# A second attention pass with the second exponential a step later and its product two steps behind

## The chip, the cores and the metric

The kernel runs on one core of a Trainium2 chip. The metric is the device time of one execution in microseconds. It was run three times (3113.05, 3113.25 and 3115.47 us); one more execution was recorded by the hardware profiler. Comparisons below are with the median, 3113.25 us.

## The reference

The program is a small perceiver of four layers. In each layer 128 query tokens of width 256 attend to a long context of 12544 tokens of width 192, then follow a self-attention and a feed-forward part. Only the context attention of layers 0 and 2 is changed. Both compute, with 16 heads of width 16 and a scale of 1/4:

```python
q = x @ Wq;  k = context @ Wk;  v = context @ Wv       # layer 2 adds bq, bk, bv
scores = einsum('bhid,bhjd->bhij', q, k) * scale
scores = where(context_mask, scores, -max)             # layer 0 only
out = einsum('bhij,bhjd->bhid', softmax(scores), v) @ Wo   # layer 2 adds bo
```

Layer 1 does the same with clipped scores, and layer 3 has wider heads and a kernel of its own. All arithmetic is in 32-bit floats.

## The kernel before, in words

`attend_twice_in` handles the context attention of layers 0, 1 and 2. It takes the heads in two groups of eight (`g`). For each group it goes over the context twice. The first pass computes the scores once to find each query's maximum (`highest`, L550 and L551) and, in between, projects the context into keys and values, which stay in SBUF. The second pass computes the scores again, subtracts the maximum, takes the exponential and multiplies by the values. A column of ones beside the values yields the softmax's sum.

The second pass has 49 steps, each of two 128-token chunks. A step has four units (`t`), each with two of the group's heads: 32 rows of the query and key tiles, so that units sit on different rows of the array. In layers 0 and 2 (`weights`, without a clip) the units are treated in two ways:

- Units 0 and 1 go into a PSUM tile of two banks, `pair`. TensorE itself adds the negative maximum (`less_maximum`, L584, in layer 2; in layer 0 the row of the mask does it too, L629). ScalarE then takes the exponential straight from PSUM (L634). I call this the early exponential.
- Units 2 and 3 go into one PSUM bank each, `one`. VectorE subtracts the maximum, and in layer 0 adds the mask, on the way to SBUF: two instructions over 512 columns in layer 2 (L289), four over 256 in layer 0 (L292). ScalarE then takes the exponential in place (L645). I call this the late exponential.

The product with the values is `weighted` (L654): eight matmuls for each half, the first half with the early exponential, the second with the late one. The profile records each of these 32-bit matmuls as two. The product of a step is issued after the scores of the next step. PSUM has two `pair` tiles (four banks), three `one` tiles and one accumulator, all eight banks.

The manager `in_order` makes TensorE, VectorE and ScalarE keep the order in which the code names the work in these passes; elsewhere a scheduler places instructions. An engine runs its instructions in order and stops at the first one whose semaphore isn't ready. Transfers are issued from queues: SP's, and at times GpSimd's.

In layer 0 a mask row is made for every four chunks, so for every two steps, which I call a block. `mask_rows` copies the mask's bytes into four partitions (L533, by SP's queue), and GpSimd turns them into a row (L535, then L537 in the second pass). There are two byte tiles for each pass and three row tiles.

After the steps of group 0, the first keys and values of group 1 are projected before the last product; after group 1 the output is transposed, normalised and projected.

Of the kernel before, what the change touches and what calls it, by code (L numbers as in the profile page):

```python
# [12 lines left out]
F32 = mybir.dt.float32  # L13
# [3 lines left out]
AF = mybir.ActivationFunctionType  # L17
# [4 lines left out]
P = 128  # L22
D = 256
# [3 lines left out]
S2 = 12544  # L27
# [9 lines left out]
RANK = 32  # L37
# [168 lines left out]
class Net:  # L206
# [222 lines left out]
    def layernorm(self, x):  # L429
        nc = self.nc  # L430
        st = self.sp.tile([P, nc.vector.BN_STATS_DIM], F32, tag="bn", name="bn")
        nc.vector.bn_stats(st, x)
        mv = self.sp.tile([P, nc.vector.BN_AGGR_DIM], F32, tag="mv", name="mv")
        nc.vector.bn_aggr(mv, st)
        r = self.stat(1)
        self.ts(r, mv[:, 1:2], 1e-5, None, ALU.add)
        nc.scalar.activation(r, r, AF.Sqrt)
        nc.vector.reciprocal(r, r)
        xn = self.ap.tile([P, D], F32, tag="xn", name="xn")
        self.ts(xn, x, mv[:, 0:1], r, ALU.subtract, ALU.mult)  # L440
        return xn

# [67 lines left out]
    def attend_twice_in(self, pool, o, qz, keys, masked, clip, between):  # L510
        nc, d = self.nc, self.d
# [3 lines left out]
        rows = []  # L515
# [10 lines left out]
        def mask_rows(b, second=False):  # L526


            src = d["mask"].rearrange("c p -> (c p)")[b * SB : min(S2, b * SB + SB)].unsqueeze(0)
            n = src.shape[-1]  # L530
            to = rows8[second][b % 2]
            at = 3 if second else 0
            nc.sync.dma_start(to[at:P:32, :n], src.to_broadcast([4, n]))  # L533
            row = pool.tile([P, SB], BF16, tag="row", name="row", bufs=3)
            nc.gpsimd.tensor_scalar(row[:, :n], to[:, :n], 0.0, 1.0, ALU.is_gt, ALU.subtract)  # L535
            if second:
                nc.gpsimd.tensor_scalar(row[:, :n], row[:, :n], self.bar, three, ALU.mult, ALU.add)  # L537
            else:
                nc.gpsimd.tensor_scalar(row[:, :n], row[:, :n], self.bar, None, ALU.mult)
            return row  # L540
# [49 lines left out]
            at = x[:, j * HB : (j + 1) * HB]  # L590
            nc.tensor.matmul(at, keys.kT(c // 4)[tiles[t], k], q, start=start, stop=True, skip_group_check=True)  # L591

        def exponentials(bufs):
            e = pool.tile([P, 2, 2, 2, P], F32, tag="e", name="e", bufs=bufs)
            return e, e.rearrange("p i j s q -> p i (j s q)")

        def weights_clipped(g, c, m, floor):
# [17 lines left out]
        def weights(g, c, m, less, row):  # L615


            pair = self.pair()
            x = [pair[:, 0, :], pair[:, 1, :], self.single(), self.single()]
            if row is None:  # L620
                for t in range(2):
                    less_maximum(t, x[t], m)
            else:
                for j in range(2):
                    at = slice(j * HB, (j + 1) * HB)
                    k = slice((c % 4 + j) * P, (c % 4 + j + 1) * P)
                    for t in range(2):
                        r = tiles[t]
                        nc.tensor.matmul(x[t][:, at], row[r, k], m[r, at], start=j == 0, stop=False, skip_group_check=True)  # L629
            for j in range(2):  # L630
                for t in range(4):
                    score(g, c, t, j, x[t], start=t >= 2 and j == 0)
            e, to = exponentials(4)
            nc.scalar.activation(to, pair, AF.Exp)  # L634
            es = [e]
            e, to = exponentials(4)
            for i in range(2):
                by_chunk = x[2 + i].rearrange("p (j n) -> p j n", j=2)
                dest = to[:, i].rearrange("p (j n) -> p j n", j=2)
                if row is None:  # L640
                    self.tt(dest, by_chunk, bc(less[:, i], 1, 2), ALU.add)
                    continue
                for j in range(2):
                    self.stt(dest[:, j], by_chunk[:, j], self.mask_col[:, c + j : c + j + 1], less[:, i], ALU.add, ALU.add)
            nc.scalar.activation(to, to, AF.Exp)  # L645
            return es + [e]

        def weighted(g, c, es, acc):

            v = keys.v(c // 4)  # L650
            for half in range(2):
                for j in range(2):
                    for t in range(4):
                        nc.tensor.matmul(  # L654
                            acc[32 * t : 32 * t + 17, half, :], v[:, c % 4 + j, 4 * half + t, :], es[half][:, t // 2, j, t % 2, :],
                            start=c + j + half == 0, stop=c + j == S2 // P - 1, skip_group_check=True,
                        )

        for g in range(2):
            if g == 0:  # L660
# [40 lines left out]
            made, lag = [], 1 if clip is None else 2  # L701
            engines = [mybir.EngineType.PE, mybir.EngineType.DVE, mybir.EngineType.Activation]
            with self.in_order(*(engines if clip is None else [])):
                for c in range(0, S2 // P, 2):
                    if clip is not None:
                        es = weights_clipped(g, c, m, floor)
                    else:
                        if masked and c % 4 == 0:
                            rows.append(mask_rows(c // 4, True))
                        es = weights(g, c, m, less, rows[-1] if masked else None)  # L710
                    made.append((g, c, es, acc))
                    if len(made) > lag:
                        weighted(*made.pop(0))
            if g == 0:
                for b in range(2):
                    for part in range(2):
                        keys.project(1, b, part)
            for step in made:
                weighted(*step)
            oT = pool.tile([P, 2, P], F32, tag="oT", name="oT", bufs=1)  # L720
            nc.vector.tensor_copy(oT, acc)
            p = self.pair()
            for half in range(2):
# [245 lines left out]
    def xattn_biased(self, x, name, guarded, keys):  # L969
        nc, d = self.nc, self.d  # L970
        with self.tc.tile_pool(name=name, bufs=2, reuse_waits="tile") as pool:
            xT = self.normed(x)
            wq = self.load_w(d[f"{name}_Wq"], 2, D, "wq")
            bq = self.load_row(d[f"{name}_bq"], D)
            bv = self.all_rows(d[f"{name}_bv"], D, "bv", pool)
            wo = self.load_w(d[f"{name}_Wo"], 2, D, "wo")
            bo = self.load_row(d[f"{name}_bo"], D)
            qz = pool.tile([P, 2, 2, P], F32, tag="qz", name="qz", bufs=1)
            for g in range(2):
                c = slice(g * P, (g + 1) * P)  # L980
# [51 lines left out]
    def prepare_l3(self, pool):  # L1032
# [25 lines left out]
        def load():  # L1058
            for j, name in enumerate("qkvo"):
                alpha = self.all_rows(d[f"L3_xattn_{name}_alpha"], 1, f"a{name}", self.sp)  # L1060
                self.ts(self.rate[:, j : j + 1], alpha, 1.0 / RANK, None, ALU.mult)
            for i, k in ((1, "k"), (2, "v")):
                down = pool.tile([RANK, 2 * P], F32, tag=f"down{k}", name="down")
                nc.sync.dma_start(down[:, :CD], d[f"L3_xattn_{k}_downT"])
                nc.sync.dma_start(down[:, CD:], d[f"L3_xattn_{k}_downT"][:, P:])
                up = pool.tile([RANK, dims], F32, tag=f"up{k}", name="up")
                nc.sync.dma_start(up, d[f"L3_xattn_{k}_up"])
                w = self.load_kv(d[f"L3_xattn_W{k}"], dims, f"w{k}", own)
                self.w3.append(w)
                parts.append(add_low(i, k, down, up, w))  # L1070
# [743 lines left out]
```

## Time and profile before

| what | us |
|---|---|
| median of three runs | 3113.25 |
| the profiled execution | 3108.01 |
| its span | 3106.3 |
| layer 0, group 0: from the first to the last early exponential's start (171.26 to 288.55) | 117.29 |
| layer 0, group 1 (447.59 to 563.97) | 116.38 |
| layer 2, group 0 (1518.64 to 1628.81) | 110.17 |
| layer 2, group 1 (1783.01 to 1890.68) | 107.67 |
| TensorE busy in these four, in that order | 111.07, 110.73, 109.92, 107.26 |
| ScalarE busy in these four | 94.63, 94.54, 94.70, 94.62 |
| VectorE busy in these four | 79.70, 79.71, 62.02, 61.92 |
| GpSimd busy in these four | 65.26, 58.23, 0, 0 |

A group in the profile is a line with an engine, an operation and its tiles. After the bar stand its busy time in us and the mean of one in ns; after the second bar the idle time of the engine just before these instructions, and what ended most of it. In the timeline a line has its start, its duration, engine, line, operation, tiles and count; square brackets hold the idle time before it. The chain of waits is followed back from the last instruction to whatever released each one; its lines have a start, a duration, and what ran. PE is TensorE, PEld its weight loads, DVE VectorE, ACT ScalarE, POOL GpSimd. The end of a matmul is modelled, so starts are the better witnesses.

### The profile page before, as it was taken

To read this page: it belongs to the slowest core of one execution; us is meant where nothing else is said; L and a number is where in the kernel's file an instruction comes from. 1 tells how busy PE (TensorE), PEld (TensorE's weight loads), DVE (VectorE), ACT (ScalarE), POOL (GpSimd) and SP (SyncE) were. 2 spreads that over 40 slices of the span, in tenths; PEclk is the share of its full clock that TensorE was granted. 3 is DMA by queue.
4 is the path that set the end of the run, shared out by engine and by line. 5 is a ranking of instruction groups with operands and counts; after the bars stand their busy time and mean duration, and the time that the engine had idled before them with its cause. 6 is when DMAs were issued, how large, how long until landed. Compare 5 with 4: busy or idle time off the path is not lost.

```text
span 3106.3 us, 78634 instructions
## 1 busy us (share of the span) xinstructions
PE 2943.0 (95%) x34877; PEld 2201.4 (71%) x34877; DVE 2249.8 (72%) x2887; ACT 1429.1 (46%) x1673; POOL 430.4 (14%) x451
## 2 busy tenths in 40 slices
PE   9999999869999999899999999899999999999979
PEld 6666656535576676675666566489889889889867
DVE  6866876638897898669657755477777777777854
ACT  1166128421284266311482185256555556556521
POOL 6645665212000000120000001000000000000000
PEclk9999999989999999899899999899999999999979
DMA  4100210551101201452102105322223232223436
GB/s 131 55 18 22 71 45 3 182 207 55 32 3 52 60 18 29 130 163 57 34 3 73 55 3 202 120 84 83 84 80 88 81 85 82 84 79 88 122 112 205
DMA packets 165659, 246.97 MB, mean 80 GB/s; under 512 B 20061, under 2 KB 107231, under 8 KB 165320
## 3 DMA queue, kind: packets, MB, share of 16 engines
q1 hardware_dynamic: 160600, 227.77, 24.1%
q0 software_dynamic: 4608, 14.16, 1.4%
q8 instruction: 274, 4.49, 0.6%
q14 instruction: 65, 0.53, 0.1%
q10 hardware_dynamic: 112, 0.01, 0.0%
HBM read 241.75 MB, written 0.13 MB: 78 GB/s over the span
## 4 chain that ended last, share of the span: by engine, by line
PE 80%; DVE 13%; ACT 4%; issue 2%; DMA 1%; POOL 0%; SPq 0%; ACTq 0%; DVEq 0%; POOLq 0%
PE pair L102 20%; PE pair L550 10%; PE v L102 8%; PE acc L654 6%; PE sc L774 6%; PE acc L816 6%; PE ps L278 5%; PE pair L591 5%; DVE e L292 4%; DVE parts L551 3%; PE acc L278 2%; PE kv L102 2%; PE one L591 2%; ACT e L645 2%; PE pair L584 2%
## 5 line engine op out<-in xcount | busy, mean ns | idle before, releaser
L551 DVE TENSOR_REDUCE parts<-pair 128x2 f32<-128x1024 f32 x600 | 679.2, 1198 | 104.4 <-PE pair L550 104.2
L102 PE MATMUL pair<-ctxA,wk 128*128 128x256 f32 x1236 | 328.9, 399 | 1.4 <-ACT kT L193 1.1
L102 PEld LDWEIGHTS pair<-ctxA,wk 128*128 128x128 f32 x1236 | 217.0, 190 | 139.9 <-DVE parts L551 96.0
L550 PE MATMUL pair<-kT,qz 32*128 32x512 f32 (+1 forms) x1632 | 277.5, 615 | 9.2 <-DVE parts L551 8.9
L289 DVE TENSOR_TENSOR top<-top,kept 128x1024 f32<-128x1024 f32 (+2 forms) x145 | 169.1, 1169 | 133.3 <-ACT kept L776 132.0
L776 ACT COPY kept<-sc 128x1024 f32<-128x1024 f32 (+1 forms) x135 | 136.2, 1009 | 259.7 <-PE sc L774 259.7
L645 ACT ACTIVATE e<-e 128x1024 f32<-128x1024 f32 x196 | 207.2, 1057 | 72.6 <-DVE e L292 45.6
L292 DVE SCALAR_TENSOR_TENSOR e<-pair,floor 128x1024 f32<-128x1024 f32 x196 | 230.5, 1219 | 8.3 <-PE pair L591 2.3
L654 PE MATMUL acc<-e,v 128*17 128x128 f32 x6336 | 221.5, 274 | 11.6 <-ACT e L645 10.2
L611 ACT ACTIVATE e<-e 128x1024 f32<-128x1024 f32 x196 | 207.2, 1057 | 40.0 <-DVE e L292 32.5
L292 DVE SCALAR_TENSOR_TENSOR e<-one,maskcol,less 128x256 f32<-128x256 f32 x392 | 162.6, 477 | 78.5 <-PE pair L591 51.4
L591 PE MATMUL pair<-qz,kT 32*128 32x256 f32 x2112 | 219.4, 374 | 0.0
L535 POOL TENSOR_SCALAR row<-mask 128x512 bf16<-128x512 uint8 (+1 forms) x100 | 189.3, 1894 | 209.9 <-PE pair L629 106.4
L654 PEld LDWEIGHTS acc<-e,v 128*17 128x17 f32 x6336 | 145.1, 97 | 97.2 <-issue 42.5
L634 ACT ACTIVATE e<-pair 128x1024 f32<-128x1024 f32 x196 | 197.4, 1007 | 33.0 <-PE pair L591 32.4
L132 ACT ACTIVATE kT<-pair,bk 128x512 f32<-128x512 f32 (+1 forms) x68 | 45.9, 675 | 348.1 <-PE pair L102 348.1
L774 PE MATMUL sc<-qz,kT 64*128 64x128 f32 x2816 | 197.8, 279 | 0.0
L289 DVE TENSOR_TENSOR e<-one,less 128x512 f32<-128x512 f32 x196 | 126.4, 686 | 95.4 <-PE pair L591 92.9
L102 PEld LDWEIGHTS v<-wv,ctxA 128*128 128x128 f32 x1568 | 190.5, 192 | 6.6 <-issue 1.7
L102 PE MATMUL v<-wv,ctxA 128*128 128x128 f32 x1568 | 193.8, 276 | 0.0
L102 PE MATMUL pair<-ctxB,wk 64*128 64x256 f32 x1236 | 188.4, 398 | 0.0
L774 PEld LDWEIGHTS sc<-qz,kT 64*128 64x128 f32 x2816 | 171.6, 187 | 13.0 <-issue 1.3
(438 smaller groups left out, 5465.3 us busy)
## 6 DMA issues: line engine op xcount, KB each, us to landing
ctxA<-in_ctxA SPq DMA_DIRECT2D x324, 256.0 KB
ctxB<-in_ctxB SPq DMA_DIRECT2D x339, 128.0 KB
w<-in_L_ffn_W SPq DMA_DIRECT2D x32, 1024.0 KB
ctxA<-in_ctxA POOLq DMA_DIRECT2D x36, 256.0 KB, 3.4
w<-in_L_ffn_w_gateT SPq DMA_DIRECT2D x8, 1024.0 KB
wu<-in_L_ffn_w_upT SPq DMA_DIRECT2D x8, 1024.0 KB
w<-in_L_ffn_w_downT SPq DMA_DIRECT2D x8, 1024.0 KB
w<-in_L_ffn_w1T SPq DMA_DIRECT2D x8, 1024.0 KB
```

What stands on the lines that cost most here:

```text
L102: self.nc.tensor.matmul(out, a, b, start=start and not low, stop=low == 1, skip_group_check=True)
L278: self.nc.tensor.matmul(out, lhsT, rhs, start=(i == 0), stop=(i == n - 1))
L289: self.nc.vector.tensor_tensor(out, a, b, op)
L292: self.nc.vector.scalar_tensor_tensor(out, a, s, b, op0, op1, **kw)
L550: nc.tensor.matmul(x[:, i, :n], qz[r, g, s, :], keys.kT(b)[r, :n], start=not masked, stop=True)
L551: nc.vector.tensor_reduce(parts[:, s, 2 * half : 2 * half + 2, b], x[:, :, :n], AX.X, ALU.max)
L591: nc.tensor.matmul(at, keys.kT(c // 4)[tiles[t], k], q, start=start, stop=True, skip_group_check=True)
L611: nc.scalar.activation(to, to, AF.Exp)
L634: nc.scalar.activation(to, pair, AF.Exp)
L645: nc.scalar.activation(to, to, AF.Exp)
L654: nc.tensor.matmul(acc[32 * t : 32 * t + 17, half, :], v[:, c % 4 + j, 4 * half + t, :], es[half][:, t // 2, j, t % 2, :], start=c + j + h ...
L774: nc.tensor.matmul(x[:, t, c : c + P], kT[r, c : c + P], qz[r, g, :], start=True, stop=True)
```

## The change

In layers 0 and 2 the late exponential of a step is issued after the early exponential of the next step. The product of a step is split: its first half follows the scores of the next step, its second half those of the step after that. The sums of VectorE get SBUF tiles of their own tag, `late`, three of them; the early exponentials keep two. The second pass's mask bytes go by GpSimd's queue. Some tiles give up room: `xn` has one buffer, the attention's output before the transposition (`oT`) takes the place of `low`, `bv` has one buffer, and two pairs of small matrices for layer 3 (`down`, `up`) share one tile each, on different partitions. Layer 1 keeps its order. What is computed stays the same.

```diff
-            nc.sync.dma_start(to[at:P:32, :n], src.to_broadcast([4, n]))
+            (nc.gpsimd if second else nc.sync).dma_start(to[at:P:32, :n], src.to_broadcast([4, n]))
...
-            e, to = exponentials(4)
+            e, to = exponentials(2)
             nc.scalar.activation(to, pair, AF.Exp)
             es = [e]
-            e, to = exponentials(4)
+            e, to = exponentials(3, "late")
...
-            nc.scalar.activation(to, to, AF.Exp)
             return es + [e]
+
+        def late_exponential(step):
+            to = step[1][1].rearrange("p i j s q -> p i (j s q)")
+            nc.scalar.activation(to, to, AF.Exp)
...
-                        es = weights(g, c, m, less, rows[-1] if masked else None)
-                    made.append((g, c, es, acc))
-                    if len(made) > lag:
-                        weighted(*made.pop(0))
+                    made.append((c, weights(g, c, m, less, rows[-1] if masked else None)))
+                    if n > 0:
+                        late_exponential(made[n - 1])
+                        weighted(0, *made[n - 1], acc)
+                    if n > 1:
+                        weighted(1, *made[n - 2], acc)
+                if clip is None:
+                    late_exponential(made[-1])
             if g == 0:
                 for b in range(2):
                     for part in range(2):
                         keys.project(1, b, part)
-            for step in made:
-                weighted(*step)
-            oT = pool.tile([P, 2, P], F32, tag="oT", name="oT", bufs=1)
+            if clip is not None:
+                weighted(0, *made[-2], acc)
+            weighted(1, *made[-2], acc)
+            for half in range(2):
+                weighted(half, *made[-1], acc)
+            oT = pool.tile([P, 2, P], F32, tag="low" if clip is None else "oT", name="oT", bufs=1)
...
-        xn = self.ap.tile([P, D], F32, tag="xn", name="xn")
+        xn = self.ap.tile([P, D], F32, tag="xn", name="xn", bufs=1)
...
-            bv = self.all_rows(d[f"{name}_bv"], D, "bv", pool)
+            bv = pool.tile([P, D], F32, tag="bv", name="bv", bufs=1)
+            nc.sync.dma_start(bv, d[f"{name}_bv"].to_broadcast([P, D]))
...
+            downs = pool.tile([2 * RANK, 2 * P], F32, tag="down", name="down")
+            ups = pool.tile([2 * RANK, dims], F32, tag="up", name="up")
             for i, k in ((1, "k"), (2, "v")):
-                down = pool.tile([RANK, 2 * P], F32, tag=f"down{k}", name="down")
+                at = slice((i - 1) * RANK, i * RANK)
+                down, up = downs[at], ups[at]
...
-                up = pool.tile([RANK, dims], F32, tag=f"up{k}", name="up")
```

More of the change, by code (lines that the diff above doesn't have):

```diff
@@ L591, in score, with exponentials @@
             nc.tensor.matmul(at, keys.kT(c // 4)[tiles[t], k], q, start=start, stop=True, skip_group_check=True)
-        def exponentials(bufs):
-            e = pool.tile([P, 2, 2, 2, P], F32, tag="e", name="e", bufs=bufs)
+        def exponentials(bufs, tag="e"):
+            e = pool.tile([P, 2, 2, 2, P], F32, tag=tag, name="e", bufs=bufs)
             return e, e.rearrange("p i j s q -> p i (j s q)")
@@ L644, in weights, with weighted @@
                     self.stt(dest[:, j], by_chunk[:, j], self.mask_col[:, c + j : c + j + 1], less[:, i], ALU.add, ALU.add)
+            return es + [e]
+        def late_exponential(step):
+            to = step[1][1].rearrange("p i j s q -> p i (j s q)")
             nc.scalar.activation(to, to, AF.Exp)
-            return es + [e]
-        def weighted(g, c, es, acc):
+        def weighted(half, c, es, acc):
             v = keys.v(c // 4)
[L651 to L657, printed above, removed]
+            for j in range(2):
+                for t in range(4):
+                    nc.tensor.matmul(
+                        acc[32 * t : 32 * t + 17, half, :], v[:, c % 4 + j, 4 * half + t, :], es[half][:, t // 2, j, t % 2, :],
+                        start=c + j + half == 0, stop=c + j == S2 // P - 1, skip_group_check=True,
+                    )
         for g in range(2):
@@ L700, in attend_twice_in @@
             nc.vector.memset(acc, 0.0)
-            made, lag = [], 1 if clip is None else 2
+            made = []
+            steps = range(0, S2 // P, 2)
             engines = [mybir.EngineType.PE, mybir.EngineType.DVE, mybir.EngineType.Activation]
             with self.in_order(*(engines if clip is None else [])):
-                for c in range(0, S2 // P, 2):
+                for n, c in enumerate(steps):
                     if clip is not None:
[L706 to L709, printed above, removed]
-                        es = weights(g, c, m, less, rows[-1] if masked else None)
-                    made.append((g, c, es, acc))
-                    if len(made) > lag:
-                        weighted(*made.pop(0))
+                        made.append((c, weights_clipped(g, c, m, floor)))
+                        if n > 1:
+                            for half in range(2):
+                                weighted(half, *made[n - 2], acc)
+                        continue
+                    if masked and c % 4 == 0:
+                        rows.append(mask_rows(c // 4, True))
+                    made.append((c, weights(g, c, m, less, rows[-1] if masked else None)))
+                    if n > 0:
+                        late_exponential(made[n - 1])
+                        weighted(0, *made[n - 1], acc)
+                    if n > 1:
+                        weighted(1, *made[n - 2], acc)
+                if clip is None:
+                    late_exponential(made[-1])
             if g == 0:
@@ L717, in attend_twice_in @@
                         keys.project(1, b, part)
-            for step in made:
-                weighted(*step)
-            oT = pool.tile([P, 2, P], F32, tag="oT", name="oT", bufs=1)
+            if clip is not None:
+                weighted(0, *made[-2], acc)
+            weighted(1, *made[-2], acc)
+            for half in range(2):
+                weighted(half, *made[-1], acc)
+            oT = pool.tile([P, 2, P], F32, tag="low" if clip is None else "oT", name="oT", bufs=1)
             nc.vector.tensor_copy(oT, acc)
```

## The prediction

> **What bounds the kernel now.** I read the busy shares first, then the costliest groups, then the chain of waits inside one second pass, then TensorE's timeline over one pair of steps. TensorE is busy 95% of the span, so the question is which of its remaining gaps lie in the four passes that change. The groups of those passes:
>
> ```profile
> PE 2943.0 (95%) x34877; PEld 2201.4 (71%) x34877; DVE 2249.8 (72%) x2887; ACT 1429.1 (46%) x1673; POOL 430.4 (14%) x451
> ...
> L645 ACT ACTIVATE e<-e 128x1024 f32<-128x1024 f32 x196 | 207.2, 1057 | 72.6 <-DVE e L292 45.6
> L654 PE MATMUL acc<-e,v 128*17 128x128 f32 x6336 | 221.5, 274 | 11.6 <-ACT e L645 10.2
> ```
>
> The late exponential (L645) idles for VectorE's sum, and the value product (L654) idles for the late exponential. The chain of waits in layer 0's first second pass, here one turn of it:
>
> ```profile
> 224.86 1.67 DVE e L292 x4
> ...
> 226.61 1.07 ACT e L645
> ...
> 227.72 0.63 PE acc L654 x16
> 228.35 0.21 PE pair L629 x2
> ...
> 229.71 1.67 DVE e L292 x4
> ```
>
> One turn is VectorE, ScalarE, half a product, one step's scores, VectorE again: 229.71 - 224.86 = 4.85 us. Only every second VectorE unit appears: a turn covers two steps, so a step costs 2.42, whatever TensorE could do. TensorE's own timeline over that pair:
>
> ```profile
> 226.85 0.63 PE L654 MATMUL acc<-e,v 128*17 128x128 f32 x16
> 227.72 0.63 PE L654 MATMUL acc<-e,v 128*17 128x128 f32 x16 [0.25 <-ACT e L645]
> 228.29 0.28 PE L629 MATMUL pair<-low,row 32*128 32x256 bf16 x2
> 229.47 1.07 PE L654 MATMUL acc<-e,v 128*17 128x128 f32 x32
> 230.48 0.28 PE L629 MATMUL pair<-low,row 32*128 32x256 bf16 x2
> 230.50 0.48 PE L591 MATMUL one<-qz,kT 32*128 32x256 f32 x1
> 230.64 0.48 PE L591 MATMUL one<-qz,kT 32*128 32x256 f32 x1
> 231.69 0.63 PE L654 MATMUL acc<-e,v 128*17 128x128 f32 x16
> ```
>
> In the step that begins at 228.29 the product runs unbroken (x32): 1.18 from step start to product, 1.01 of product, 2.19 in all. In its neighbours the second half waits for the late exponential: 226.85 to 228.29 is 1.44 instead of 1.0. The early exponentials (L634) in the timeline alternate 2.66, 2.19. Layer 2 has the same form with a shorter VectorE unit (1.29 instead of 1.66); its early exponentials alternate 2.29, 2.18, so only 0.11 in two steps is lost.
>
> **What the Trainium skill says.** "TensorE: Matmul & The Clock Gate", Part 1 (the clock gate): after an idle stretch the array runs at half clock until about 3.4 us of activity. The trace agrees: granted clock 0.56 in 445 to 450 us, at a pass's start, and 1.00 in every 5 us from 450 on. So the floor of a step is the full-clock one, and the first steps are priced apart. "DMA: Bandwidth & Descriptors", Anatomy of one DMA: about 2.0 us fixed for a transfer that GpSimd issues; the trace has more, 2.8/3.4/7.0 (min/median/max) to landing for GpSimd's context loads. The same page, SWDGE vs HWDGE vs iDMA: VectorE's 2-port mode can lock GpSimd out while it writes descriptors; "VectorE: DVE Perf Modes", Mode 2x_2P, says that mode needs SBUF operands and a single tensor. Here VectorE's pass work reads PSUM and adds a second tensor, so I expect no lock; no run yet shows it.
>
> **The change, part by part.**
>
> *Late exponential a step later, its product two behind.* Per step TensorE now does scores(n), first half of product n-1, second half of product n-2. Nothing is added or removed: 16 product matmuls a step still, two exponentials on ScalarE, the same VectorE work. What goes is the wait. With T the end of scores(n): VectorE's unit n runs T+0.05 to T+1.7; ScalarE has exp(n) from T+0.05, then the late one of n-1, done by T+2.05. That is wanted after scores(n+1) and half a product, T+2.2+0.5: slack 0.65. The late one of n starts after exp(n+1), near T+3.2, when VectorE has been done for 1.5. ScalarE's start-to-start times are 0.97 (226.61 to 227.58) and 0.90 (1550.35 to 1551.25), 1.87 a step, under 2.19. So TensorE sets the step.
>
> What is late next: the PSUM singles. There are three, two used a step, so a step's second single needs the first single of the step before, free after two of VectorE's four instructions. VectorE starts 1.42 after the step's start (228.29 to 229.71), and the wait above shows the release at 230.64, 0.93 later; the single was wanted at 230.50. That 0.14 moved the product only from 1.18 to 1.21 after the step's start, as other row groups went on. With unbroken products every layer 0 step meets this: 1.21 + 1.0 = 2.21. In layer 2 VectorE's first half is 0.69 and the step is 2.18.
>
> *Buffers.* Early tiles 2, late tiles 3 instead of 4 shared. VectorE's late tile n is the one of n-3, whose product ends just before scores(n); the early tile of n-2 likewise. Covered by the 1.2 of scores; 0.
>
> *Ends.* The first steps have less product, the last ones more. With a loop behind the pass (group 0) half a product, 0.5, moves behind it. In group 1 the last late exponential stands behind two others: it starts 0.97 + 0.96 after the last early one, against 1.70 now in layer 0 (563.97 to 565.67) and 1.32 in layer 2 (1890.68 to 1892.00): +0.2 and +0.6.
>
> *Mask by GpSimd's queue.* 50 transfers leave SP's queue (0.52 each), which is idle then apart from them; behind them stand context loads and, after group 1, the next stage's weights (563.88), which wait for TensorE anyway. On GpSimd they are issued two blocks ahead, right after the row two blocks earlier. GpSimd's cost per block (two steps): 1.92 + 0.77 for the row, 0.1 between, plus 0.54 of issue (its context loads' median): 3.4 of 4.4. Unknown is the issue of this shape; taken 0.54, between 0.5 and 2 (SP's 0.52 to about the skill's fixed cost), hidden either way. Landing has two blocks less that, 8.8 - 3.4 = 5.4, and rows are made some four steps before use:
>
> ```profile
> 226.12 1.92 POOL L535 TENSOR_SCALAR row<-mask 128x512 bf16<-128x512 uint8 x1 [2.05 <-PE pair L629]
> 228.14 0.77 POOL L537 TENSOR_SCALAR row<-row,bar,three 128x512 bf16<-128x512 bf16 x1
> 230.96 1.92 POOL L535 TENSOR_SCALAR row<-mask 128x512 bf16<-128x512 uint8 x1 [2.05 <-PE pair L629]
> ```
>
> GpSimd waits 2.05 in each block for TensorE to free a row. Two such issues (1.1) also go to the program's start, where GpSimd idles 4.5 for the mask; 0. Without cover they would be 1.1.
>
> *The rest* (one xn, oT in the place of low, shared down/up tiles, own bv) keeps every instruction; order on VectorE and on TensorE outside the passes is unchanged. 0; if a shared tile made someone wait, about 1 us each, once.
>
> **The sum**, from first to last early exponential (48 intervals), against the profiled execution. Layer 0, group 0: 117.3 now; then 2.1 + 2.0 for the first two (VectorE and a cold clock set them), 46 x 2.21 = 101.7, and 0.6 for the one irregular step: 106.4, less 10.9, plus 0.5 tail = -10.4. Group 1: 116.4 to 2.1 + 2.0 + 101.7 = 105.8, plus 0.2 = -10.4. Layer 2, group 0: 110.2 to 2.3 + 3.4 (half a cold product, 0.9, gone from 4.28) + 46 x 2.18 = 100.3 + 0.6 = 106.6, plus 0.5 = -3.1. Group 1: 107.7 to 2.7 + 1.7 + 100.3 = 104.7, plus 0.6 = -2.4. Together -26.3: 3108.0 becomes 3081.7. The median of the runs, 3113.25, lies 5.2 above the profiled execution; the saving carried over gives 3087.0.
>
> **Rivals.** *The PSUM single is the new bound.* If the 0.14 wait came through whole, a layer 0 step would be 2.33: 92 x 0.12 = 11 less saved, -15, 3098. For it: the wait is in every second step now, and in all of them after. Against: those steps reach their product 0.03 late, not 0.14. *ScalarE paces it, so that nothing is gained.* In its queue an early exponential waits for scores and the late one stands behind it. It needs over 2.43 a step; 1.87 is measured, and even its two durations end to end are 2.07. Then 3113 within 6. *GpSimd's rows fall behind: slower.* Place: layer 0's row loop. TensorE's mask matmul waits for the row, and everything stands behind it. Layer 2 would still give 5.5, so it decides at a block time of 4.85 + 5.5/49 = 4.96, an issue above some 2.1 us, or a landing that is not covered. With landing exposed, 2.8 + 0.54 + 3.4 = 6.7 a block: 49 x 1.9 = +93, less 5.5, near 3200. For it: GpSimd never carried these. Against: two blocks of prefetch, and 2.05 of spare time.
>
> **How the numbers follow.** Forecast 0.72; single 0.15; ScalarE 0.06; rows 0.07. Faster by over 0.2% (6 us, about what can be told here) 0.87, same 0.06, slower 0.07. The low end has layer 0 steps at 2.19 (-1.8), the irregular steps absorbed (-1.2) and 2 for the spread of the runs: 3082. The high end takes in the single rival with 1 us: 3099.
>
> **What would show it.** Right: early exponentials evenly 2.2 apart in layer 0 and 2.18 in layer 2; the product's wait for the late exponential near nothing; TensorE's wait on singles of 0.1 in every layer 0 step; GpSimd still waiting for TensorE, about 1 us a block. Wrong: an idle of the mask matmul before GpSimd's row; a layer 0 step at 2.3 or more; alternation that remains; a transfer after layer 0 that now ends last.

## The result, and the profile after

The changed kernel takes 3082.51 us (median of four runs, 3080.96 to 3084.20), the kernel before, run beside it, 3114.36 (3113.05 to 3119.38). The ratio is 0.9895, with a 95% interval of 0.9878 to 0.9912. Forecast were 3087.0 and a range of 3082 to 3099. Against the 3113.25 of the forecast the ratio makes 3080.6, so the direction was right and the forecast saving of 26.3 was 5 to 6 us too small. The profiled execution took 3080.96 us with a span of 3079.3, 27.0 under the span before.

The busy shares and the groups of the passes after; a group's columns are busy time, mean ns of one instruction, and the idle time before them with what ended it:

```profile
PE 2923.5 (95%) x34877; PEld 2212.8 (72%) x34877; DVE 2249.7 (73%) x2887; ACT 1428.3 (46%) x1673; POOL 456.7 (15%) x501
...
L658 PE MATMUL acc<-e,v 128*17 128x128 f32 x6336 | 211.4, 274 | 3.1 <-ACT e L651 2.2
...
L651 ACT ACTIVATE e<-e 128x1024 f32<-128x1024 f32 x196 | 205.1, 1048 | 0.0
```

The late exponential (now L651) had an idle time of 72.6 us, and has none. The value product (now L658) waits 2.2 us for it instead of 10.2. The chain of waits in layer 0's first second pass no longer leaves TensorE:

```profile
223.48 1.00 PE acc L658 x32
224.48 0.21 PE pair L631 x2
...
225.67 1.00 PE acc L658 x32
226.67 0.21 PE pair L631 x2
...
227.88 1.00 PE acc L658 x32
```

Two steps take 227.88 - 223.48 = 4.40 us, against 4.85 before, and ScalarE and VectorE are out of the chain. TensorE's timeline of the same stretch (start, duration, matmuls in the group) shows what remains:

```profile
223.41 1.07 PE L658 MATMUL acc<-e,v 128*17 128x128 f32 x32
224.41 0.28 PE L631 MATMUL pair<-low,row 32*128 32x256 bf16 x2
...
225.60 1.07 PE L658 MATMUL acc<-e,v 128*17 128x128 f32 x32
226.60 0.28 PE L631 MATMUL pair<-low,row 32*128 32x256 bf16 x2
226.62 0.48 PE L592 MATMUL one<-qz,kT 32*128 32x256 f32 x1
...
226.76 0.48 PE L592 MATMUL one<-qz,kT 32*128 32x256 f32 x1
...
227.81 1.07 PE L658 MATMUL acc<-e,v 128*17 128x128 f32 x32
```

The products shown here run unbroken (x32). They start 2.19 and then 2.21 apart; in the longer step the second score into a single comes 0.14 after the first instead of 0.10 as in its neighbour (224.44 and 224.54). In layer 2 the products start 2.18 to 2.19 apart (1835.60, 1837.79, 1839.97). GpSimd's timeline of the same pass has the new issue and a spare 1.05 in every block:

```profile
224.91 1.93 POOL L536 TENSOR_SCALAR row<-mask 128x512 bf16<-128x512 uint8 x1 [1.05 <-PE pair L631]
226.94 0.76 POOL L538 TENSOR_SCALAR row<-row,bar,three 128x512 bf16<-128x512 bf16 x1
227.66 0.61 POOL L534 DMA_DIRECT2D mask<-in_mask  x1
```

The four passes, from first to last early exponential, in us, and the head of the program up to the first of these:

| trace | layer 0, g 0 | layer 0, g 1 | layer 2, g 0 | layer 2, g 1 | sum | head |
|---|---|---|---|---|---|---|
| before | 117.3 | 116.4 | 110.2 | 107.7 | 451.5 | 171.3 |
| forecast | 106.4 | 105.8 | 106.6 | 104.7 | 423.5 | 171.3 |
| after | 105.4 | 107.9 | 106.5 | 104.4 | 424.3 | 179.8 |

In these two traces the passes explain the whole difference of 27.0. But the head is 8.6 longer after, and something else gave that back. A part of each pass is drawn, too: its second interval is about 2 us at TensorE's full clock and about 4 at half clock (4.28 in layer 2, g 0, before; 3.96 and 4.05 in layer 0, g 1, and layer 2, g 0, after). That, and the 31 to 32 us between the medians, is what the experiments had to explain.

### The profile page after: what moved, and what is told of

It reads as the page before. It is cut to its first block, busy times and chain, and to the rows that moved or that the text cites. A ratio compares the mean times of both kernels' runs of the same rounds, so it can differ in the third digit from the quotient of the medians.

```text
span 3079.3 us, 78420 instructions
## 1 busy us (share of the span) xinstructions
PE 2923.5 (95%) x34877; PEld 2212.8 (72%) x34877; DVE 2249.7 (73%) x2887; ACT 1428.3 (46%) x1673; POOL 456.7 (15%) x501
## 4 chain that ended last, share of the span: by engine, by line
PE 79%; DVE 14%; issue 2%; ACT 2%; DMA 2%; POOL 1%; SPq 0%; DVEq 0%; ACTq 0%; POOLq 0%
PE pair L102 20%; PE pair L551 10%; PE acc L658 8%; PE v L102 7%; PE sc L790 6%; PE acc L832 5%; PE pair L592 4%; PE ps L278 4%; PE one L592 4%; DVE parts L552 3%; DVE e L292 2%; PE kv L102 2%; PE acc L278 2%; PE pair L585 2%; PE ps L1624 1%
## 5 line engine op out<-in xcount | busy, mean ns | idle before, releaser
L552 DVE TENSOR_REDUCE parts<-pair 128x2 f32<-128x1024 f32 x600 | 679.3, 1197 | 108.2 <-PE pair L551 108.0
L536 POOL TENSOR_SCALAR row<-mask 128x512 bf16<-128x512 uint8 (+1 forms) x100 | 189.6, 1896 | 173.7 <-PE pair L551 102.5
L658 PE MATMUL acc<-e,v 128*17 128x128 f32 x6336 | 211.4, 274 | 3.1 <-ACT e L651 2.2
L651 ACT ACTIVATE e<-e 128x1024 f32<-128x1024 f32 x196 | 205.1, 1048 | 0.0
L658 PEld LDWEIGHTS acc<-e,v 128*17 128x17 f32 x6336 | 155.8, 97 | 67.9 <-ACT e L651 45.6
```

What stands on the lines that cost most here:

```text
L552: nc.vector.tensor_reduce(parts[:, s, 2 * half : 2 * half + 2, b], x[:, :, :n], AX.X, ALU.max)
L658: nc.tensor.matmul(acc[32 * t : 32 * t + 17, half, :], v[:, c % 4 + j, 4 * half + t, :], es[half][:, t // 2, j, t % 2, :], start=c + j + h ...
```

## The experiments

**Is it drawn, or is it the mask's queue?** Four kernels: both kernels unchanged once more, the changed kernel with the mask back on SP's queue, and the kernel before with the mask alone moved. The edit of the third is shown; the fourth is its reverse on the kernel before.

```diff
-            (nc.gpsimd if second else nc.sync).dma_start(to[at:P:32, :n], src.to_broadcast([4, n]))
+            nc.sync.dma_start(to[at:P:32, :n], src.to_broadcast([4, n]))
```

The kernel before again:

> The kernel before, unchanged, against itself: what executions differ by. Scatter theory (the four passes save about 27 us, as the two profiles show; what the medians show beyond that is TensorE's clock in other stages and the draw of executions): ratio 1.000 with an interval of about 0.1 to 0.2% either side, and a profile whose four passes again take 117.3, 116.4, 110.2 and 107.7 us to within 1 us, while the first 170 us and the stages between differ by some us. Queue theory (GpSimd's queue saves the extra 5 us): the same here, and all executions of the kernel before near 3114.

The changed kernel again:

> The changed kernel, unchanged, in more rounds and with a second profile. Scatter theory: 27 to 32 us less than before, the four passes at 105.4, 107.9, 106.5 and 104.4 to within 2 us, layer 0's steps again alternating 2.19 and 2.22; the half clock at 24 to 33 us and at 158 to 182 us of the first profile need not return, and where it does not, the first early exponential of layer 0 starts near 171 us rather than 180. Rival (the change itself delays the start of layer 0): it starts near 180 again.

The changed kernel with SP's queue:

> The change without the mask's move: its bytes go by SP's queue as before. Scatter theory: the same time as the changed kernel to within 3 us, 27 to 32 less than before. Queue theory: 5 us slower than the changed kernel, 26 less than before.

The kernel before with GpSimd's queue:

> The kernel before with the mask's move alone. Scatter theory: the same time as before to within 3 us. Queue theory: 5 us less than before. If GpSimd's queue were slow: more than before, rows late, TensorE's mask matmul idle for them.

| kernel | us | ratio, 95% | passes | head |
|---|---|---|---|---|
| before again | 3112.09 | 0.9997 [0.9987, 1.0007] | 449.3 | 173.3 |
| after again | 3082.42 | 0.9899 [0.9884, 0.9915] | 420.2 | 174.5 |
| after, mask by SP | 3081.91 | 0.9893 [0.9878, 0.9909] | 425.0 | 171.7 |
| before, mask by GpSimd | 3106.49 | 0.9975 [0.9966, 0.9983] | 450.9 | 174.4 |

The difference of about 30 us repeats. Not every pass came as expected: layer 2's first took 108.0 instead of 110.2 in the kernel before, and layer 0's second 105.6 instead of 107.9 in the changed kernel, since no second interval of a pass was at half clock in these two traces. That makes them the cleaner pair: 449.3 - 420.2 = 29.1 us saved in the passes. In the changed kernel the queue decides nothing: 3082.42 and 3081.91. Yet in the kernel before the queue alone gave 7 us, with passes as they were. The queue theory held for one kernel and failed for the other, so neither theory was complete.

**Which half of the order brings it, and which layer?** First the late exponential back in its old place, with its product still two steps behind:

```diff
+            nc.scalar.activation(to, to, AF.Exp)
             return es + [e]
...
                     if n > 0:
-                        late_exponential(made[n - 1])
                         weighted(0, *made[n - 1], acc)
...
-                if clip is None:
-                    late_exponential(made[-1])
```

> The changed kernel, but ScalarE's late exponential is back in its old place, right behind VectorE's sums of the same step; the late half's product stays two steps behind. Product theory (what removes the wait is that TensorE asks for the late exponential a step later; where ScalarE computes it doesn't matter as long as it is done 1.9 us before it is asked for): steps 2.21 in layer 0 and 2.18 in layer 2, passes 423 us together from first to last early exponential, time 3082 within 3. ScalarE theory (the late exponential in its old place makes the next early one start up to 0.55 late, since it waits for VectorE with the early one behind it, and the early half's product, one step behind, waits for that): layer 0 steps at 2.3 or more, passes 431 or more, time 3090 or more.

It takes 3083.36 us (ratio 0.9901 [0.9886, 0.9916]), passes 423.3, steps 2.20 to 2.22 in layer 0 and 2.18 in layer 2: the same as the changed kernel. The product's place does all the work. Then the reverse, the late exponential a step later and both halves of the product one step behind:

```diff
-                        weighted(0, *made[n - 1], acc)
-                    if n > 1:
-                        weighted(1, *made[n - 2], acc)
+                        for half in range(2):
+                            weighted(half, *made[n - 1], acc)
...
```

> The changed kernel, but both halves of the product one step behind, while the late exponential stays a step later. The product then waits for a late exponential that starts only behind the next early one and ends 2.05 after the scores: step 2.05 + 0.55 + 1.2 = 3.8 in both layers, 192 steps with 1.37 to 1.6 more than before: about +285, 3400. If ScalarE's place doesn't matter to the product, no slower than before: 3113 or less.

It takes 3411.46 us (1.0952 [1.0931, 1.0973]), passes 752.0. TensorE's timeline of this kernel in layer 0's first second pass:

```profile
223.20 0.63 PE L658 MATMUL acc<-e,kv 128*17 128x128 f32 x16 [1.57 <-ACT e L651]
...
227.15 0.63 PE L658 MATMUL acc<-e,kv 128*17 128x128 f32 x16 [1.57 <-ACT e L651]
```

The cut between the lines leaves out the first half of the product. The wait that the change removes comes back as 1.57 before the second half in each step, and a step is 227.15 - 223.20 = 3.95, a little over the 3.8 expected. So the later exponential by itself costs 300 us; it is harmless only because its product is later still. Then the new order in one layer at a time, which for layer 0 alone reads:

```diff
+                    if not (masked):
+                        late_exponential(made[n])
+                        if n > 0:
+                            for half in range(2):
+                                weighted(half, *made[n - 1], acc)
+                        continue
...
```

> The new order of late exponential and product in layer 0's two passes alone; layer 2 in the old order, in the changed kernel's buffers; mask by GpSimd, all else as in the changed kernel. Passes' theory: layer 0's passes 105.4 to 108, layer 2's 107.7 to 110.2 as before; time 3113.4 less 20 to 21 plus whatever the parts outside the passes give (0 to -5): 3088 to 3093. If the extra 4 us beyond the passes come with the order itself, this is 3093; if with the small edits around it or with the mask's queue, 3088.

> The new order in layer 2's two passes alone; layer 0 in the old order within the changed kernel's buffers, mask by GpSimd. Passes' theory: layer 2's passes 104.4 each, layer 0's 117.3 and 116.4 as before; time 3113.4 less 5 to 7: 3107, or 3102 if the small edits or the mask's queue bring their own 4 to 7 us. A time at 3113 would mean that layer 2's steps had no wait to lose.

Layer 0 alone: 3085.80 (0.9910 [0.9895, 0.9926]). Layer 2 alone: 3103.26 (0.9960 [0.9946, 0.9974]). Layer 0 alone went below its expected 3088 to 3093; layer 2 alone came close to the 3102 expected if the edits around the order bring their own part. The traces hold a surprise: the steps of the layer left in the old order are faster than before. Layer 0's in the second kernel are 2.40, not 2.43 to 2.45, and layer 2's in the first are 2.21, not 2.24 to 2.26. (Layer 0's passes in the second kernel are not shorter as a whole, 117.6 and 117.3, since the second interval of both was at half clock, 4.54 and 4.11.)

**What do the other edits do?** The changed kernel with the old order in both layers and the mask on SP's queue, so with the new buffers and small edits alone (the branch above, taken for both layers):

> Both layers in the old order and the mask on SP's queue, but with the changed kernel's buffers and small edits (early tiles 2 and late tiles 3 apart, one xn, oT in low's place, own bv by a broadcast, shared down and up tiles). My account of the prediction (these edits cost and bring nothing; the 4 us by which the change beat the forecast lie in TensorE's clock outside the passes): 3113 within 2, passes 450.5. Rival (the small edits bring the missing 4 us): 3109 or below, passes unchanged.

It takes 3102.94 us (0.9961 [0.9946, 0.9975]), passes 442.6. My account, that these edits bring nothing, is false. The rival, that they act outside the passes, is false too as it stood: the passes are 8 to 9 shorter, and 6.7 shorter than the 449.3 of the trace of the kernel before that, like this one, has no second interval at half clock. The chain of waits shows why. First the kernel before, between VectorE's sums and the late exponential that begins at 226.61:

```profile
224.86 1.67 DVE e L292 x4
226.53 0.02 issue
226.55 0.02 ACTq L645
226.57 0.04 issue
```

Then the kernel with the buffers and small edits alone:

```profile
225.06 1.67 DVE e L292 x4
226.73 0.02 issue
226.75 1.07 ACT e L651
```

From the end of the sums to the exponential it is 0.08 in the first and 0.02 in the second. In the compiled program the late exponential of the kernel before waits for two semaphores, VectorE's and one of ScalarE itself; with three late tiles of their own instead of four shared ones the second wait is gone. Each turn of the old chain contained this once, so two steps went from 4.85 to 4.79.

Next, the kernel before with one small edit, the shared tiles of the down and up matrices; and with all small edits, but the exponentials' four tiles shared as before:

```diff
+            downs = pool.tile([2 * RANK, 2 * P], F32, tag="down", name="down")
+            ups = pool.tile([2 * RANK, dims], F32, tag="up", name="up")
             for i, k in ((1, "k"), (2, "v")):
-                down = pool.tile([RANK, 2 * P], F32, tag=f"down{k}", name="down")
+                at = slice((i - 1) * RANK, i * RANK)
+                down, up = downs[at], ups[at]
...
-                up = pool.tile([RANK, dims], F32, tag=f"up{k}", name="up")
```

> The kernel before with one edit of the change: the down and up matrices share one tile each. Table-load theory (this edit moves addresses, so that the exponential of gains in the stage behind layer 0 waits for VectorE alone and not also for ScalarE; the wait then stands at the activation and not at the table load before it, which is 1.28 us off the path; TensorE's idle stretch there falls from 1.9 to 1.0 us and its clock isn't halved for the 10 us behind it): that stage 51.0 becomes 46 to 47, passes 450.5, time 3113.5 less 4 to 5.5: 3108 to 3109.5. Rival (the stage is shorter for another part of the change, or by the drawing of clock phases): stage 51, time 3113.5.

> The kernel before with all the small edits (one xn, oT in low's place, own bv, shared down and up tiles), but the exponentials' four tiles shared as before; order and mask as before. Two-part theory (the small edits shorten the stages outside the passes, the separate late tiles shorten the passes by taking a second wait, the one on ScalarE itself, off the late exponential): passes 450.5 again, stages as with all edits, time 3113.5 less 4 to 7, so 3107 to 3110, and the 3103 of the run with the separate tiles are 4 to 7 lower. Rival (it is the small edits that shorten the passes too): passes 442.6, time 3103.

Shared tiles alone: 3101.55 (0.9957 [0.9942, 0.9972]), passes 449.5. All small edits: 3102.34 (0.9961 [0.9947, 0.9975]), passes 451.6. The 451.6 hold one second interval of 4.54, so without half clock both are near 449. So the shorter passes belong to the separate tiles of the exponentials, as the two-part theory says; but the small edits gave 11 to 12 where it expected 4 to 7, and the shared tiles alone as much where 4 to 5.5 were expected. And all small edits together gave no more than one of them. That can't be a sum of pieces of work.

**Drawn or made: the stages outside the passes.** I then read TensorE's granted clock. Two stages stand out. One is the stage behind layer 0's context attention (571 to 623 us in the trace before), the other the one with the feed-forward's narrow matmuls behind layer 2 (1938 to 2003 us). Two more traced executions each of the kernel before, of the shared tiles alone, and of the mask alone:

> The kernel before, another execution. If the edit decides: stage behind layer 0 51.0, the later stage 63.9 again. If the later stage is drawn: 59 to 60 in some of these looks, 64 in others; the stage behind layer 0 stays at 51.0.

> The kernel before, another execution; as for the first look at it: 51.0 behind layer 0; 63.9 in the later stage if the edit decides, 59 to 60 or 64 if it is drawn.

> The kernel before with the shared down and up tiles alone, another execution. Stage behind layer 0 45 to 47 in either case. The later stage: 59 to 60 if the edit decides, 64 in some looks if it is drawn.

> The kernel with the shared down and up tiles alone, another execution; as for the first look at it: 45 to 47 behind layer 0; 59 to 60 in the later stage if the edit decides, 64 in some looks if it is drawn.

> The kernel before with the mask alone on GpSimd's queue, another execution. Head up to the first early exponential 173.5 or more (171.1 to 173.4 with SP's queue), passes 451, stage behind layer 0 51.0. If the 7 us lie in TensorE's clock elsewhere: two or three of layer 1's stage (546 instead of 549) and about 4 of the later stage (59 to 60 instead of 64). If they lie in the passes: 444.

> The same kernel in one more execution, with the same expectations: head 173.5 or more, passes 451, stage behind layer 0 51.0; layer 1's stage 546 and the later stage 59 to 60 if the clock brings the 7 us; passes 444 if they do.

| traces | behind layer 0 | behind layer 2 | head |
|---|---|---|---|
| before, four | 51.0 to 51.1 | 63.9 to 64.0 | 171.3 to 173.4 |
| mask by GpSimd alone, three | 51.1, 45.7, 51.2 | 63.9, 63.6, 59.9 | 174.4, 173.7, 179.6 |
| shared tiles alone, three | 45.5, 46.7, 46.6 | 59.7, 63.7, 63.7 | 171.1 to 172.2 |
| changed kernel, two | 45.2, 45.7 | 59.9, 63.7 | 179.8, 174.5 |

The mask alone didn't do as expected: its passes stay near 449 where no second interval is at half clock (448.9 and 448.6), so its 7 us don't lie in them; but the stage behind layer 0 was shorter in one of the two executions and the stage behind layer 2 in the other.

The stage behind layer 2 is drawn: one and the same kernel shows about 60 and about 64. Windows over it in the kernel with the shared tiles; the third number from the right is the granted clock. One execution, of the shorter stage:

```profile
1955.58:1963.58 8.00, 5.14 (x50) 2.02 (x46) 3.25 (x9) 2.75 (x5) 0.00 (x0) 0.79 0.64 226
1963.58:1971.58 8.00, 7.92 (x98) 3.01 (x90) 3.47 (x9) 2.22 (x6) 0.00 (x0) 1.00 1.02 380
```

Another execution of it, of the longer stage:

```profile
1959.10:1967.10 8.00, 5.39 (x38) 2.08 (x38) 2.75 (x7) 2.57 (x5) 0.00 (x0) 0.63 0.66 217
1967.10:1975.10 8.00, 8.00 (x60) 2.27 (x52) 1.57 (x4) 1.06 (x3) 0.00 (x0) 0.52 1.00 360
```

In the second windows, eight equally full microseconds, TensorE gets through 98 matmuls or through 60, at clock 1.00 or 0.52.

The stage behind layer 0 looked like the edit's own, since all thirteen traces with the shared tiles have 45.2 to 47.0. I had a cause for it: in the kernel before, ScalarE's table load of 1.28 us stands behind VectorE, and with the shared tiles ahead of it. (The Trainium skill, "ScalarE: Activation LUTs", What ACT_TABLE_LOAD costs, gives about 1.28 us for the load, as measured here.) In ScalarE's timeline of the kernel with the mask alone, the load waits for VectorE:

```profile
589.89 1.28 ACT L475 ACT_TABLE_LOAD   x1 [1.15 <-DVE gains L289]
```

In the changed kernel it doesn't:

```profile
574.34 1.28 ACT L475 ACT_TABLE_LOAD   x1
```

TensorE's idle behind it is 1.88 to 2.04 in the seven traces with the load in the old place. In seven of the thirteen with the shared tiles it is 0.8 to 1.1; in the six others no idle of that length stands there, and a shorter stretch at half clock, 3.4 us, stands before it.

The executions with the mask alone show that this story lacks a part. Both have the table load in the old place and the same idle of TensorE behind it. First the execution with 45.7, in TensorE's timeline:

```profile
595.51 1.10 PE L278 MATMUL ps<-qkv,wide 128*128 128x512 f32 x2 [1.93 <-DVE coef L292]
```

The windows of this execution around that idle:

```profile
591.21:594.62 3.41, 2.37 (x14) 1.81 (x12) 3.06 (x10) 0.32 (x1) 1.80 (x2) 1.00 1.07 355
594.62:598.04 3.42, 2.53 (x6) 0.89 (x6) 3.25 (x21) 0.00 (x0) 0.67 (x2) 1.00 1.05 403
```

The execution with 51.2, in TensorE's timeline:

```profile
599.74 1.12 PE L278 MATMUL ps<-qkv,wide 128*128 128x512 f32 x2 [1.90 <-DVE coef L292]
```

And its windows:

```profile
597.27:600.68 3.41, 1.51 (x8) 0.67 (x6) 3.41 (x18) 0.00 (x0) 2.24 (x3) 1.00 1.05 367
600.68:604.09 3.41, 3.41 (x7) 1.15 (x6) 3.24 (x16) 0.00 (x0) 0.00 (x0) 0.50 1.06 393
...
610.92:614.33 3.41, 3.41 (x17) 2.19 (x16) 2.77 (x12) 0.00 (x0) 1.22 (x2) 1.00 1.02 381
```

After an idle of 1.93 the clock stayed at 1.00, after one of 1.90 it fell to half for 10.24 us. The edges of these windows are taken from the traces' own record of the clock: in each of the twenty traces every stretch at half clock begins on one grid with a step of 3.41 us, and the grid lies elsewhere in each execution. In the execution with 51.2 the idle falls whole into one step of the grid, in which TensorE is busy for 1.51 us (the first number after the comma), and the clock falls at its end. In the one with 45.7 a grid point at 594.62 splits the idle, and TensorE is busy for 2.37 and 2.53 in the two steps. The other five traces with 51.0 to 51.2 have the idle whole in one step, busy for 40 to 45%. Over all twenty traces, 287 of 308 steps at full clock in which TensorE was busy for less than half (the first 5 us left out) were followed by a step at half clock, and 70 of 14623 in which it was busy for over nine tenths. The Trainium skill says of the gate ("TensorE: Matmul & The Clock Gate", Part 1) that it watches a free-running window of activity, so that what it does varies from run to run. The traces agree, with 3.41 us for the window.

So the 5 us of this stage are half clock. Where the table load stands goes together with how long TensorE idles, and the grid decides whether the idle costs anything: half clock followed it in six of the seven traces with the load in the old place, and in none of the seven in which the load stands ahead and the idle is 0.8 to 1.1. That the load's place alone makes the idle longer is not shown, since no run moved the load by itself.

**The executions at equal clock.** Each run has a mean granted clock. Over 73 executions of the kernel before, the time falls by 2.0 us for each 0.001 of it (correlation -0.82): 3112.2 at 0.965. Set against that line, the kernels differ by:

| kernel | executions | mean clock | median us | against the line |
|---|---|---|---|---|
| before | 73 | 0.9639 | 3113 | 0 |
| changed | 8 | 0.9654 | 3082.5 | -28.6 ± 0.7 |
| changed, mask by SP | 4 | 0.9657 | 3081.9 | -29.5 ± 0.5 |
| changed, exponential in its old place | 4 | 0.9648 | 3083.4 | -29.5 ± 1.2 |
| layer 0 alone | 5 | 0.9666 | 3085.8 | -23.0 ± 0.5 |
| layer 2 alone | 10 | 0.9648 | 3103.3 | -9.8 ± 0.6 |
| buffers and small edits alone | 6 | 0.9660 | 3102.9 | -8.4 ± 0.6 |
| all small edits alone | 7 | 0.9683 | 3102.3 | -3.1 ± 0.5 |
| shared tiles alone | 6 | 0.9695 | 3101.6 | -1.9 ± 1.0 |
| mask by GpSimd alone | 17 | 0.9678 | 3106.5 | +0.7 ± 0.8 |

(The ± is the standard error of the mean; the line itself is a fit, so the last digits shouldn't be leaned on.) At equal clock the mask's queue leaves nothing, and the shared tiles next to nothing. The buffers and small edits give 8.4, of which the small edits have 3.1, so that some 5 are left for the separate tiles; their passes showed 6.7. The kernels with the new order in one layer contain those tiles in the other layer, too, so their two gains overlap: 23.0 + 9.8 - 8.4 = 24.4. The whole change has 28.6, so the pieces fit to some 4 us and no better. The line takes all half clock to cost the same wherever it falls, which is not shown. What remains is that the small edits, and the mask's queue, move the mean clock, by 0.004 to 0.006 in the kernel before; the whole change moves it by 0.0015 (± 0.0005).

**The PSUM single.** Last, the changed kernel with VectorE's four sums in another order, so that the single that the next scores want is free 0.42 later:

```diff
-                for j in range(2):
+            for j in range(0 if row is None else 2):
+                for i in range(2):
...
```

> The changed kernel, but VectorE's four sums of a layer 0 step in the order first chunk of both singles, then second chunk of both, so the single that the next scores want is freed 0.42 later; layer 2 as it is. If a wait for the single is absorbed up to 0.11 and beyond that moves the product one for one (my reading: 0.14 late costs 0.03): layer 0 steps 2.21 + 0.42 = 2.63, time 3082 + 92 x 0.42 = 3121 within 6. If singles don't pace the scores at all: 2.21 and 3082.

It takes 3097.61 us (0.9951 [0.9934, 0.9969]), between the two expectations. Layer 2's steps stay at 2.18, layer 0's are 2.40 on average. The products' starts in TensorE's timeline:

```profile
223.43 1.07 PE L660 MATMUL acc<-e,v 128*17 128x128 f32 x32
...
226.02 1.07 PE L660 MATMUL acc<-e,v 128*17 128x128 f32 x32
...
228.23 1.07 PE L660 MATMUL acc<-e,v 128*17 128x128 f32 x32
...
230.82 1.07 PE L660 MATMUL acc<-e,v 128*17 128x128 f32 x32
```

Steps alternate 2.59 and 2.21. In a step that has been held up, VectorE starts as early as in the other (at 223.64 and 225.85, 1.42 after the mask matmuls that open the steps at 222.22 and 224.43), while the step itself is 0.38 longer, so the next one finds its single free. So a wait for a single does reach the product once it is past what is absorbed (0.38 of the 0.42), but only in every second step. Expected in each of them, it was overpriced by 23 us (3121 against 3097.61).

## Why the prediction was right or wrong

**Late exponential a step later, its product two behind: right.** The products are unbroken, the wait for the late exponential is gone, and TensorE sets the step. The four passes were forecast 28.0 shorter from first to last early exponential; the first two traces say 27.2, and the two without a second interval at half clock 29.1. What the text didn't separate is that the exponential's own place is immaterial once the product is two steps behind: 3083.36 with it in its old place.

**What is late next: right in size.** Layer 0's steps are 2.20 to 2.21 in the changed kernel, the forecast 2.21, layer 2's 2.18. But the wait appears in every second step (0.14 instead of 0.10 between the singles), not as 0.1 in each, so what was to show it came only in part. The rival of the PSUM single is refuted for this kernel, and the last experiment shows that it would have become real with 0.42 more.

**Ends: right.** From the last early exponential's start to the end of the last late one it was 566.73 - 563.97 = 2.76 in layer 0, group 1, and is 555.69 - 552.77 = 2.92: +0.16, forecast +0.2. In layer 2 it went from 2.38 to 2.91, +0.53, forecast +0.6. The half products behind the passes of group 0 were not measured by themselves.

**Buffers: no wait, as priced, but a gain was overlooked.** In the old order the separate late tiles are worth 5 to 7 us, by taking a wait for ScalarE itself off the late exponential. In the new order the chain doesn't go through that exponential, so this should be inside the saving and not add to it; the new order with the exponentials' four tiles shared was not run, so that is argued and not shown.

**Mask by GpSimd's queue: right in the passes, incomplete at the start.** GpSimd waits 1.05 a block, close to the forecast of about 1, with an issue of 0.61 instead of the 0.54 taken. None of the 50 issues took over 0.75, so no sign of a lock by VectorE shows. At the program's start the two issues take 1.33 and fall into GpSimd's wait for the mask, as the prediction said. But other small work of GpSimd is then left until after the first mask row: from the first to the third row's end it is 7.1 in all ten traces with the mask on SP's queue, and 7.7 in all ten with it on GpSimd's. The head was 171.1 to 173.4 in the former and 173.5 to 180.8 in the latter; in the three longest (179.6 to 180.8) TensorE had 17 us at half clock from 160 to 182 us, in the others 7 or 14. How much of the longer head comes from the late rows is not shown. At equal clock none of it shows in the time.

**The rest, and the sum: here the prediction failed.** The step that failed is the 0 for the rest ("keeps every instruction; order [...] unchanged"). The work is nearly the same (-1.9 ± 1.0 and -3.1 ± 0.5 at equal clock). But alone these edits lower the median by 11 to 12 us, through the clock that TensorE is granted in stages outside the passes. One of them is located: behind layer 0, 45.2 to 47.0 instead of 51.0. In the whole change this stage is as short (45.2 and 45.7), some 5 us that the sum didn't have, and the 10.24 us at half clock that it has lost are worth 0.5 x 10.24 / 3106 = 0.0016 of mean clock, as much as the whole shift of 0.0015; but other stages, the head above all, vary by as much from execution to execution. The sum then carried the saving over from one execution to a median of others as if the clock were the same in both, with 2 us allowed for the spread. By the line, the higher mean clock is worth 3 us, and the work gave 28.6 instead of 26.3. (That these two make the measured 31 to 32 is no proof, since the line divides what was measured.) Of the 2.3 that the work gave more, 1.1 lies in the passes, 29.1 instead of 28.0; the rest is not located.

**Rivals.** ScalarE as the pace is refuted: from 200 to 280 us in the changed kernel TensorE is busy for all 80.00 us and ScalarE for 71.53, and layer 0's early exponentials each wait at least 0.21 for TensorE. The rows falling behind are refuted by GpSimd's 1.05 of spare time; the size of that rival counted the issue twice, in the 0.54 and in the 3.4, so 6.2 a block and +66 would have been meant.

What stays open is why these edits shift the mean clock by more than one stage explains: the shared tiles by 0.0056 in the kernel before, the mask's queue by 0.0039. With the whole change together less of it is left.

## What to carry to other kernels

When an engine in order waits for a result of the step before, move the consumer a step back, and check the tile that the next producer needs; here the consumer's place was worth nearly all of it, and the producer's place alone cost 300 us. In a kernel with stages that go in and out of TensorE's half clock, compare variants at equal mean clock before giving a few us to any edit: an edit that does nothing in the passes can be worth 7 to 12 us of a median, and it doesn't add up with the next one. Price the queue's start, too, and not only its steady state.

## What the runs showed of the hardware

- TensorE's clock fell to half for 10.24 us after an idle of 1.90 us in one execution and stayed full after one of 1.93 in another of the same kernel; the difference was 5 us in a stage of 46.
- In all twenty traces, stretches at half clock begin on a grid of 3.41 us that lies elsewhere in each execution. The first idle fell into one step of it (TensorE busy for 1.51 us), the second into two (2.37 and 2.53).
- Time and mean granted clock go together over executions of one kernel, 2.0 us for each 0.001 in 3113, and builds that differ in whether two pairs of small tiles share room have different mean clocks (0.9639 and 0.9695).
- A second semaphore in a late exponential's wait showed as an instruction of ScalarE's sequencer and 0.06 us more between release and start (0.08 instead of 0.02).
- GpSimd issued a mask transfer in 0.61 us during the passes, and two in 1.33 at the program's start.
